# Attention and a linear layer in one kernel: scores and values in four 64x64 array tiles, the causal mask by 64 tokens, fixed score banks, and merged rotations of q and k

## The chip, the core and the metric

The kernel runs on one core of a Trainium2 chip. The metric is the device time of one execution in microseconds; times of several runs are given as their median. The engines of the core are TensorE (PE, with its weight loads shown apart as PEld), VectorE (DVE), ScalarE (ACT), GpSimd (POOL) and SyncE (SP). SP issues most of the DMA transfers, and a transfer that has to wait holds up those behind it on the same queue. PSUM is the memory that matrix products are written into.

## The reference, cut to what matters

The hidden states have 4 sequences of 512 tokens with 1024 features; there are 16 heads of 64. All is float32.

```
q, k, v = x @ Wq.T, x @ Wk.T, x @ Wv.T          # split into 16 heads of 64
q, k = rope(q), rope(k)                          # t * cos + rotate_every_two(t) * sin
scores = where(causal, q @ k.T, -1e9) / sqrt(64) # 512 x 512 per head
attn = softmax(scores) @ v
x = layernorm(x + attn @ Wout.T)
x = layernorm(x + x @ (int8 weight * scale).T)
```

## The kernel before

**Units.** The attention part works in 32 units: a unit u is one sequence b and one pair of heads hp. Units 0 to 15 alternate between sequences 0 and 1 over the eight pairs of heads; units 16 to 31 alternate between sequences 2 and 3, with the pairs of heads in falling order. Weights are therefore loaded and split every second unit.

**Products.** q, k and v of a unit are three products (number 0, 1, 2), transposed: 128 rows (two heads of 64) by 512 tokens. To keep float32 accuracy, operands are split into a high part, a low part and a third part d, and each product is 24 matmuls of 512 columns, called tickets: 16 go into one PSUM bank A (high and low parts), 8 into a bank D. ACT scales A into `tA` (line 295) and DVE adds D to it (line 318): for q and k the result is `raw`, for v it is `v`. The pool `pj` has two banks, so A and D of successive products alternate on them, and D of one product has to wait until the DVE step of line 318 of the product before has read its D.

**Rotation.** For q and k, `swap` (line 249) makes a copy `rot` of `raw` with neighbouring rows exchanged, by two DMAs that SP issues. `rope` then runs three steps on DVE (lines 235, 236, 242): `rot * sin`, `raw * cos`, and their sum into `qk`. Before, these are 512 columns each, once for q and once for k. In units of even number the rotation of the next unit's q is done late in the unit, in odd ones it stands between the softmax parts of the unit (`slot` in `product`); that of k is in the slot "turn".

**One unit of the loop.** The loop over u records, in this order: the scores of u (line 409), their masks and maxima on DVE (lines 427 and 430), the exponentials on ACT (444), the reciprocal of the sums on DVE (452), the normalisation on POOL (458), and 72 tickets, which are product 1 and 2 of unit u + 1 and product 0 of unit u + 2. After 18 tickets come the values of unit u - 1 (`attend`, line 490), copied by ACT out of PSUM (498) and sent by a DMA on ACT's own queue to the DRAM buffer `ao` (499). Row blocks i = 0 to 3 of 128 tokens form three groups: blocks 0 and 1, block 2, block 3. For each group DVE transposes the probabilities in blocks of 32x32 (`turn`, line 463), SP writes them to the DRAM buffer `turned` (464) and reads them back into `prT` in the order that the values need (472). v is turned the same way (`turned_v`, `va`). A read back of `turned` waits until its write has landed.

**Array tiles before.** Scores use tiles of 64 rows by 128 columns: the two heads of a unit lie in the upper and the lower 64 rows, and two such matmuls run side by side. Block i multiplies 128 queries with (i + 1) * 128 keys, so causality is by 128 tokens. Values use tiles of 128 rows by 64 columns, the two heads side by side in the columns. The score tiles and the value tile come from one pool of three buffers of two banks, `pdp`. A mask of 128x128 is added to the diagonal block, by DVE, or on TensorE in the units 0, 30 and 31 (`BUSY`).

**Order.** Within the loop the order of PE, DVE and ACT is that of the program text, written out by hand. Work on SP and POOL is put in order by a scheduler. `later(u, slot, f)` puts work into a named slot of unit u; `run(u, slot)` issues it. The slots of a unit stand in this order: early, between, then, after, first, turn, mid, second, late, end. Splits of weights are DVE steps in the slots between, first and late.

After the loop come the output product (line 199), layer norms, and the last linear layer (676) over 16 tiles of 128 rows.

Of the kernel before, what the change touches and what calls it, by code (L numbers as in the profile page):

```python
# [9 lines left out]
FP = mybir.dt.float32  # L10
# [15 lines left out]
SCALE = 0.125  # L26
MASKED = -3.0e38

# [10 lines left out]
def attention_ffn_kernel(  # L39
# [28 lines left out]
    pds = ExitStack()  # L68
    pdp = pds.enter_context(tc.tile_pool(name="pd", bufs=3, space=PSUM))

    ident = const.tile([P, P], FP, name="ident")
    mask, unit = (const.tile([P, P], BF, name=name) for name in ("mask", "unit"))
    cos_sb = const.tile([P, 2, S], FP, name="cos_sb")
# [6 lines left out]
    for n in (512, 384):  # L80
        nc.tensor.matmul(warm[:, :n], lhsT=sin_sb[:, 0, :P], rhs=sin_sb[:, 0, :n], start=True, stop=True)

    make_identity(nc, ident)
    make_identity(nc, unit)
    nc.gpsimd.memset(mask, 0.0)
    nc.gpsimd.affine_select(
        out=mask,
        in_=mask,
        pattern=[[-1, P]],
        compare_op=ALU.is_ge,  # L90
        fill=MASKED,
        base=0,
        channel_multiplier=1,
    )
    nc.gpsimd.memset(eps_sb, EPS)
# [133 lines left out]
    with tc.tile_pool(name="raw", bufs=2) as rawp, tc.tile_pool(name="qk", bufs=2) as qkp, ExitStack() as heads:  # L229
        def rope(u, k):  # L230

            raw, rot = prod.pop((u, k)), prod.pop(("rot", u, k))
            if u not in qk:
                qk[u] = qkp.tile([P, 2, S], FP, tag="qk", name=f"qk_{u}")
            nc.vector.tensor_mul(rot, rot, sin_sb[:, k, :])
            nc.vector.tensor_mul(raw, raw, cos_sb[:, k, :])
            out = qk[u][:, k, :]
            if k == 0:

                out = out.rearrange("p (i r s) -> p r i s", i=NI, r=R)  # L240
                raw, rot = (t.rearrange("p (r i s) -> p r i s", i=NI, r=R) for t in (raw, rot))
            nc.vector.tensor_add(out, raw, rot)  # L242

        def swap(u, k):

            raw = prod[u, k]
            rot = prod["rot", u, k] = rawp.tile([P, S], FP, tag="rot", name=f"rot_{u}_{k}", bufs=2)
            for p in range(2):
                nc.sync.dma_start(out=rot[p::2, :], in_=raw[1 - p :: 2, :])

        def raw_tile(u, k):
            tag = "v" if k == 2 else "raw"
            t = prod[u, k] = rawp.tile([P, S], FP, tag=tag, name=f"{tag}_{u}_{k}", bufs=1 if k == 2 else 2)
            return t

# [12 lines left out]
        def product(u, k, n):  # L268
# [48 lines left out]
            if n == NT - 1:  # L317
                nc.vector.scalar_tensor_tensor(raw_tile(u, k), ps, -X12, prod["tA"], op0=MUL, op1=ADD)  # L318
                if k < 2:
                    swap(u, k)  # L320
                    slot = ("first" if last else "between" if u % 2 else "late") if k == 0 else "turn"
                    later(u - 1, slot, lambda: rope(u, k))

# [68 lines left out]

        probs, prT, stats, s_ps = {}, {}, {}, {}

        def scores(u):
            nmx = st1.tile([P, 2 * NI], FP, tag="nmx", name=f"nmx_{u}")
            den = st1.tile([P, 2 * NI], FP, tag="den", name=f"den_{u}")
            rden = st1.tile([P, 2 * NI], FP, tag="rden", name=f"rden_{u}")
            stats[u] = nmx, den, rden
            t = qk.pop(u)  # L400
            keys = t[:, 1, :].rearrange("p (r s) -> p r s", r=R)
            for g, blocks in enumerate(GROUPS):
                ps = pdp.tile([P, 2, 512], FP, tag="d", name=f"s_{u}_{g}")
                s_ps[u, g] = ps
                for i, at in blocks:
                    n = (i + 1) * P
                    for j in range(2):
                        rows = slice(j * D, (j + 1) * D)
                        nc.tensor.matmul(  # L409
                            ps[:, j, at : at + n],  # L410
                            lhsT=t[rows, 0, ts(i, P)],
                            rhs=keys[rows, :, : (i + 1) * Q],
                            start=True,
                            stop=u not in BUSY,
                        )
                    if u in BUSY:
                        diag = ps[:, :, at : at + n].rearrange("p a (r s) -> p a r s", r=R)[:, :, :, ts(i, Q)]
                        for j in range(2):
                            nc.tensor.matmul(diag[:, j], lhsT=unit, rhs=mask, start=False, stop=True)

        def maxima(u, g):
            nmx, den, rden = stats[u]
            ps = s_ps[u, g]
            for i, at in () if u in BUSY else GROUPS[g]:
                diag = ps[:, :, at : at + (i + 1) * P].rearrange("p a (r s) -> p a r s", r=R)[:, :, :, ts(i, Q)]
                tri = mask.rearrange("p (r s) -> p r s", r=R).unsqueeze(1).to_broadcast([P, 2, R, Q])
                nc.vector.tensor_tensor(diag, diag, tri, ADD)
            for i, at in GROUPS[g]:
                n = (i + 1) * P
                nc.vector.tensor_reduce(  # L430
                    nmx[:, 2 * i : 2 * i + 2], ps[:, :, at : at + n], AX.X, ALU.max, negate=True
                )

        def softmax(u, g):
            nmx, den, rden = stats[u]
            ps = s_ps.pop((u, g))
            blocks = GROUPS[g]
            pr = prp.tile([P, R, WIDE[g], 2, Q], FP, tag=f"pr{g}", name=f"pr_{u}_{g}")
            probs[u, g] = pr
            for i, at in blocks:  # L440
                n = (i + 1) * P
                for j in range(2):
                    m = 2 * i + j
                    nc.scalar.activation(  # L444
                        pr[:, :, at // P : at // P + i + 1, j, :],
                        ps[:, j, at : at + n].rearrange("p (r k s) -> p r k s", r=R, s=Q),
                        AF.Exp,
                        bias=nmx[:, m : m + 1],
                        accum_out=den[:, m : m + 1],
                    )  # L450
            i0, i1 = blocks[0][0], blocks[-1][0] + 1
            nc.vector.reciprocal(rden[:, 2 * i0 : 2 * i1], den[:, 2 * i0 : 2 * i1])  # L452
            for i, at in blocks:
                n = (i + 1) * P
                for j in range(2):
                    m = 2 * i + j
                    p = pr[:, :, at // P : at // P + i + 1, j, :]
                    nc.gpsimd.tensor_scalar(p, p, rden[:, m : m + 1], 1.0, ALU.mult, ALU.mult)  # L458

        def turn(t, d):  # L460

            t = t.rearrange("p r k j s -> p (r k j s)") if len(t.shape) > 2 else t
            nc.vector.transpose(t, t)  # L463
            nc.sync.dma_start(out=d.rearrange("a (n r) w -> (a n) (r w)", r=R), in_=t)
# [12 lines left out]
        def turn_values(u):  # L477

            rows = turn(prod.pop((u, 2)), turned["v"])
            va[u] = vap.tile([P, NI, R, Q], FP, tag="va", name=f"va_{u}")  # L480
# [3 lines left out]
        def attend(u):  # L484
            b, hp = units[u]
            ps = pdp.tile([P, 2, 512], FP, tag="d", name=f"o_{u}")[:, 0, :]
            t, v = prT.pop(u), va.pop(u)
            for kb in range(NI):
                for j in range(2):
                    nc.tensor.matmul(  # L490
                        ps[j * D : (j + 1) * D, kb * P :],
                        lhsT=v[:, kb, 2 * j : 2 * j + 2, :].rearrange("p a s -> p (a s)"),
                        rhs=t[:, :, 4 * kb : 3 * (NI - 1) + kb + 1 : 3, j, :].rearrange("p a i s -> p i a s"),
                        start=(kb == 0),
                        stop=(kb == NI - 1),
                    )
            o = otp.tile([P, S], FP, tag="ot", name=f"ot_{u}")
            nc.scalar.copy(o, ps)
            nc.scalar.dma_start(out=ao[b][:, hp, :], in_=o)

        with tc.manual_schedule(
# [60 lines left out]
            later(0, "first", lambda: split_w(0))  # L564
            later(0, "late", lambda: (diff_x(0, 3), rope(1, 0)))

# [5 lines left out]
            for u in range(NU):  # L572
# [13 lines left out]
                second = 8 if u < NU - 1 else 6  # L586
                transposes(u, 0)
                take(second)
                transposes(u, 1)
# [17 lines left out]
                run(u, "end")  # L607
            attend(NU - 1)
    pds.close()


    w8p = ctx.enter_context(tc.tile_pool(name="w8", bufs=1))
    wfv = w8p.tile([P, NC, E], FR, name="wf")
    sc32 = w8p.tile([P, E], FP, name="sc32")
# [157 lines left out]
```

## Time and profile before

| | |
|---|---|
| median of 3 runs | 1020.42 us (1020.23 to 1020.58) |
| span of the profiled execution | 1020.7 us |
| PE busy | 999.7 us |
| DVE busy | 852.8 us |
| ACT busy | 389.0 us |
| POOL busy | 201.1 us |
| mean granted TensorE clock | 0.996 |
| data moved | 204.09 MB |

The profiled execution is one run. Its span is taken from its own trace, 0.3 us above the median, so sums of its rows may be set against 1020.7. A line of the timeline gives the start in us, the length, the engine, the source line, the operation and the tiles as output<-inputs; behind it stands in brackets how long the engine had been idle and what released it. The letter q behind an engine's name marks its DMA queue.

The steady units of the loop run from scores to scores in 21.45 us. The first scores begin at 33.4 us. Units 14 and 15, in which the second pair of sequences is split for the first time, take 24.10 and 22.84 us.

### The profile page before, as it was taken

Reading aid. Unit: us, or ns where it says so; the run is one execution under the profiler, and the core shown is the slowest. Engines: PE = TensorE matmul, PEld = TensorE weight load, DVE = VectorE, ACT = ScalarE, POOL = GpSimd, SP = SyncE. Lnnn points to the kernel's source line nnn. Section 1 sums busy time; section 2 is a strip of 40 time slices with the busy share of each in tenths; the row PEclk is TensorE's granted clock in tenths of the full one; section 3 lists DMA queues with packets and bytes.
Section 4 is the critical chain, followed back from the end, with each engine's and each line's share of the span. In section 5 each row is a group of like instructions: output and inputs, shape, how many; then the busy total and the mean of one; then the engine's idle time right before and its main releaser. Section 6 shows DMA issues by size and latency. Waiting matters only on the chain.

```text
span 1020.7 us, 13748 instructions
## 1 busy us (share of the span) xinstructions
PE 999.7 (98%) x4628; PEld 742.0 (73%) x4628; DVE 852.8 (84%) x1246; ACT 389.0 (38%) x841; POOL 201.1 (20%) x283
## 2 busy tenths in 40 slices
PE   9999999999999999999999999999899999999997
PEld 4667777777777667777777777776578888888885
DVE  5998888888888999788898888889877877878776
ACT  4534444354444435445344453445332122121110
POOL 0122332222322322332223322232100000000000
PEclk9999999999999999999999999999999999999999
DMA  7576676767768787576866758688635465564551
GB/s 288 170 233 220 203 234 190 263 195 223 232 193 261 250 254 227 183 253 192 253 210 206 247 173 273 217 250 278 223 108 160 124 160 143 128 168 104 145 103 62
DMA packets 264022, 204.09 MB, mean 200 GB/s; under 512 B 147600, under 2 KB 220304, under 8 KB 263824
## 3 DMA queue, kind: packets, MB, share of 16 engines
q1 hardware_dynamic: 256176, 184.60, 60.0%
q10 hardware_dynamic: 5616, 10.75, 2.9%
q0 software_dynamic: 2160, 7.87, 1.9%
q8 instruction: 37, 0.61, 0.3%
q14 instruction: 33, 0.27, 0.1%
HBM read 112.46 MB, written 73.92 MB: 183 GB/s over the span
## 4 chain that ended last, share of the span: by engine, by line
PE 85%; DMA 5%; issue 4%; DVE 4%; POOL 1%; SPq 0%; ACT 0%; DVEq 0%; POOLq 0%
PE p L276 43%; PE y L199 15%; PE f L676 11%; PE o L490 7%; PE s L409 6%; PE pw L261 2%; DMA turned<-pr 2%; DVE pr L463 1%; POOL pr L458 1%; DMA sx<-in_wo 1%; DMA prT<-turned 1%; DMA raw_x<-in_xT 1%; DVE w_l L219 1%; DMA va<-turned_v 0%; DMA turned_v<-v 0%
## 5 line engine op out<-in xcount | busy, mean ns | idle before, releaser
L458 POOL TENSOR_SCALAR pr<-pr,rden 128x128 f32<-128x128 f32 (+3 forms) x256 | 189.9, 760 | 525.9 <-DVE rden L452 414.5
L276 PE MATMUL p<-x_h,w_h 128*128 128x512 f32 x736 | 290.2, 394 | 0.0
L276 PE MATMUL p<-x_l,w_l 128*128 128x512 f32 x736 | 286.8, 390 | 0.0
L276 PE MATMUL p<-x_d,w_d 128*128 128x512 f32 x736 | 190.9, 395 | 3.1 <-DVE v L318 2.5
L276 PEld LDWEIGHTS p<-x_h,w_h 128*128 128x128 f32 x736 | 138.1, 188 | 50.3 <-issue 22.0
L444 ACT ACTIVATE pr<-s,nmx 128x128 f32<-128x128 f32 (+3 forms) x256 | 131.5, 531 | 112.6 <-DVE nmx L430 107.1
L276 PEld LDWEIGHTS p<-x_d,w_d 128*128 128x128 f32 x736 | 135.5, 188 | 36.4 <-issue 5.1
L276 PEld LDWEIGHTS p<-x_l,w_l 128*128 128x128 f32 x736 | 138.2, 188 | 28.1
L295 ACT ACTIVATE tA<-p 128x512 f32<-128x512 f32 x92 | 55.2, 600 | 218.4 <-PE p L276 218.4
L463 DVE STREAM_TRANSPOSE pr<-pr 128x768 f32<-128x768 f32 (+1 forms) x96 | 99.7, 1057 | 24.4 <-POOL pr L458 23.7
L430 DVE TENSOR_REDUCE nmx<-s 128x2 f32<-128x256 f32 (+3 forms) x128 | 101.9, 820 | 3.0
L199 PE MATMUL y<-x_l,w_l 128*128 128x512 f32 x256 | 100.1, 391 | 2.1 <-DVE w_l L219 2.1
L199 PE MATMUL y<-x_h,w_h 128*128 128x512 f32 x256 | 100.4, 392 | 0.5 <-DVE row L208 0.5
L676 PE MATMUL f<-wf,x1lo 128*128 128x512 f32 x240 | 93.6, 390 | 1.1 <-DVE x1lo L650 1.1
L676 PE MATMUL f<-wf,x1hi 128*128 128x512 f32 x240 | 93.5, 389 | 0.0
L409 PE MATMUL s<-qk 64*128 64x384 f32 (+3 forms) x512 | 80.2, 446 | 1.0 <-DVE qk L242 1.0
L490 PE MATMUL o<-prT,va 128*64 128x256 f32 (+3 forms) x512 | 77.7, 446 | 2.2 <-DMA prT<-turned 1.7
L223 DVE TENSOR_TENSOR w_d<-w_h,w_l 128x1024 fp32r<-128x1024 f32 x60 | 74.0, 1233 | 1.5
L318 DVE SCALAR_TENSOR_TENSOR raw<-p,tA 128x512 f32<-128x512 f32 x61 | 41.8, 686 | 37.1 <-PE p L276 37.0
L490 PEld LDWEIGHTS o<-prT,va 128*64 128x64 f32 x512 | 34.8, 138 | 48.6 <-issue 42.6
L199 PE MATMUL y<-x_d,w_d 128*128 128x512 f32 x256 | 64.9, 393 | 1.6 <-DVE x_d L177 1.2
L409 PEld LDWEIGHTS s<-qk 64*128 64x128 f32 x512 | 41.4, 186 | 22.4 <-issue 11.3
(112 smaller groups left out, 1162.1 us busy)
## 6 DMA issues: line engine op xcount, KB each, us to landing
turned<-pr SPq DMA_DIRECT2D x64, 384.0 KB, 3.4
rot<-raw SPq DMA_DIRECT2D x128, 128.0 KB, 2.8
turned<-pr SPq DMA_DIRECT2D x32, 512.0 KB, 4.5
prT<-turned SPq DMA_DIRECT2D x32, 512.0 KB, 5.2
prT<-turned SPq DMA_DIRECT2D x32, 384.0 KB, 3.9
turned_v<-v SPq DMA_DIRECT2D x32, 256.0 KB, 5.0
va<-turned_v SPq DMA_DIRECT2D x128, 64.0 KB, 2.6
prT<-turned SPq DMA_DIRECT2D x32, 256.0 KB, 3.3
```

The costliest lines, as they stand in the source:

```text
L199: nc.tensor.matmul(ps, lhsT=r[part][:, c, :], rhs=w[part][:, c, :], start=n in (0, 2 * NC), stop=n in (2 * NC - 1, NT - 1),)
L223: nc.vector.tensor_tensor(d, h, l, SUB)
L276: nc.tensor.matmul(ps, lhsT=w[part][:, c, :], rhs=r[part][:, c, :], start=n in (0, 2 * NC), stop=n in (2 * NC - 1, NT - 1),)
L295: nc.scalar.activation(prod["tA"], ps, AF.Copy, scale=1.0 + X12)
L318: nc.vector.scalar_tensor_tensor(raw_tile(u, k), ps, -X12, prod["tA"], op0=MUL, op1=ADD)
L409: nc.tensor.matmul(ps[:, j, at : at + n], lhsT=t[rows, 0, ts(i, P)], rhs=keys[rows, :, : (i + 1) * Q], start=True, stop=u not in BUSY,)
L430: nc.vector.tensor_reduce(nmx[:, 2 * i : 2 * i + 2], ps[:, :, at : at + n], AX.X, ALU.max, negate=True)
L444: nc.scalar.activation(pr[:, :, at // P : at // P + i + 1, j, :], ps[:, j, at : at + n].rearrange("p (r k s) -> p r k s", r=R, s=Q), AF.Ex ...
L458: nc.gpsimd.tensor_scalar(p, p, rden[:, m : m + 1], 1.0, ALU.mult, ALU.mult)
L463: nc.vector.transpose(t, t)
L490: nc.tensor.matmul(ps[j * D : (j + 1) * D, kb * P :], lhsT=v[:, kb, 2 * j : 2 * j + 2, :].rearrange("p a s -> p (a s)"), rhs=t[:, :, 4 * k ...
L676: nc.tensor.matmul(ps, lhsT=part[:, c, :], rhs=wfv[:, c, o], start=(c == 0 and part is hi), stop=(c == NC - 1 and part is lo),)
```

## The change

The order of tokens in each sequence is changed by the host: within a block of 128 tokens they are put into rows of 16 by their number modulo 4, and odd blocks have their two halves exchanged. The host puts the rows of the result back. Then:

- Scores: four tiles of 64x64 (two heads in the rows, two halves of the queries in the columns). Each half of the queries takes only the keys that it needs by steps of 64 tokens.
- Values: four tiles of 64x64 (two halves of the keys in the rows, two heads in the columns). The two halves of the keys give two sums in two banks; ACT copies the first, DVE adds the second (`attended`), and the DMA to `ao` goes to SP's queue.
- The three score buffers are allocated once; the values always use the first.
- Masks: `added` and `bounds`, one for even and one for odd blocks, are built by POOL in token order and moved into place by 32 small DMAs that POOL issues. DVE takes the minimum with `bounds`; in the units of `BUSY` TensorE adds `added`.
- q and k of a unit share one `raw` and one `rot` tile, single-buffered. One rotation over 1024 columns replaces two over 512, in the slot "turn".
- v is transposed by blocks into a new tile under the name of `tA`.
- The identity for the transposes of the last part is made after the loop.

```diff
+    ps_d = [pdp.tile([P, 2, 512], FP, name=f"s_{g}") for g in range(3)]
...
+        for masks, open_value in ((added, 0.0), (bounds, -MASKED)):
+            by_token = maskp.tile([P, 2, P], BF, tag="by_token", name="by_token")
...
+                for c in range(2):
+                    for r in range(4):
+                        at, of = 64 * c + 16 * r, 64 * (c ^ odd) + r
+                        nc.gpsimd.dma_start(out=masks[at : at + 16, odd, :], in_=by_token[of : of + 61 : 4, odd, :])
...
-        def rope(u, k):
+        def rope(u, *ks):
...
-            nc.vector.tensor_mul(rot, rot, sin_sb[:, k, :])
-            nc.vector.tensor_mul(raw, raw, cos_sb[:, k, :])
+            nc.vector.tensor_mul(rot, rot, sin_sb[:, ks, :])
+            nc.vector.tensor_mul(raw, raw, cos_sb[:, ks, :])
+            nc.vector.tensor_add(qk[u][:, ks, :], raw, rot)
...
-                    slot = ("first" if last else "between" if u % 2 else "late") if k == 0 else "turn"
-                    later(u - 1, slot, lambda: rope(u, k))
+                    if k == 1:
+                        later(u - 1, "turn", lambda: rope(u, 0, 1))
...
+                    for c in range(2):
+                        early = i * P + c * D
+                        if i % 2 != c:
+                            pieces = ((0, (i + 1) * P),)
+                        elif c == 0:
+                            pieces = ((0, early + D),)
+                        else:
+                            pieces = ((0, i * P), (early, early + D))
+                        for j in range(2):
+                            rows = slice(j * D, (j + 1) * D)
+                            for s0, s1 in pieces:
+                                nc.tensor.matmul(
+                                    ps[c * D : (c + 1) * D, j, at + s0 : at + s1],
+                                    lhsT=t[rows, 0, early : early + D],
+                                    rhs=t[rows, 1, s0:s1],
...
-                nc.vector.tensor_tensor(diag, diag, tri, ADD)
+                nc.vector.tensor_tensor(diag, diag, tri, ALU.min)
...
+                for h in range(2):
+                    for j in range(2):
+                        rows = slice(h * D, (h + 1) * D)
...
+                        if h == kb % 2:
+                            piece(kb * P, later_blocks(kb))
+                        else:
+                            c = 1 - kb % 2
+                            piece(kb * P + c * D, t[rows, 2 * c : 2 * c + 2, 4 * kb, j, :])
+                            if kb < NI - 1:
+                                piece((kb + 1) * P, later_blocks(kb + 1))
+            o = outs[u] = otp.tile([P, S], FP, tag="ot", name=f"ot_{u}")
+            nc.scalar.copy(o, ps[:, 0, :])
+
+        def attended(u):
+
+            b, hp = units[u]
+            o = outs.pop(u)
+            nc.vector.tensor_tensor(o[:, D:], values.pop(u)[:, 1, D:], o[:, D:], ADD)
+            nc.sync.dma_start(out=ao[b][:, hp, :], in_=o)
...
                 transposes(u, 0)
+                if u:
+                    attended(u - 1)
```

## The prediction

> **What bounds the kernel now.** I read the page first (busy shares, chain by engine), then the chain of waits in order of time, then one steady unit on TensorE, DVE and SyncE, then the two units that are longer than the others.
>
> ```profile
> PE 999.7 (98%) x4628; PEld 742.0 (73%) x4628; DVE 852.8 (84%) x1246; ACT 389.0 (38%) x841; POOL 201.1 (20%) x283
> PE 85%; DMA 5%; issue 4%; DVE 4%; POOL 1%; SPq 0%; ACT 0%; DVEq 0%; POOLq 0%
> ```
>
> ```profile
> 98.28 2.36 PE s L409 x16
> 100.64 4.32 PE p L276 x18
> 104.96 2.31 PE o L490 x16
> 107.27 12.46 PE p L276 x54
> ```
>
> TensorE is busy 98% of the span. The last four lines (start, length, engine) are one unit of the attention loop: 2.36 + 4.32 + 2.31 + 12.46 = 21.45 us, with no gap; scores and values are 4.67 of it, the 72 product tickets the rest. DVE at 84% is the next bound. The view by stretches of two neighbouring units and of the one unit that is far longer (length, busy PE, PEld, DVE, ACT, POOL, granted clock, DMA share, GB/s):
>
> ```profile
> 98.21:119.66 21.45, 21.45 (x105) 15.72 (x105) 17.03 (x26) 7.64 (x22) 6.12 (x8) 1.00 0.76 239
> 119.66:141.11 21.45, 21.45 (x106) 15.72 (x105) 19.39 (x28) 11.63 (x25) 5.45 (x8) 1.00 0.64 206
> 334.13:358.23 24.10, 22.06 (x106) 15.56 (x105) 23.35 (x32) 10.14 (x24) 8.58 (x8) 1.00 0.77 249
> ```
>
> The clock is 1.00 in all three, so the long unit is no matter of the clock. What makes it long shows in its timelines (start, length, engine, line):
>
> ```profile
> 355.45 0.68 DVE L318 SCALAR_TENSOR_TENSOR v<-p,tA 128x512 f32<-128x512 f32 x1
> ```
>
> ```profile
> 354.36 0.39 PE L276 MATMUL p<-x_l,w_l 128*128 128x512 f32 x1
> 356.19 2.11 PE L276 MATMUL p<-x_d,w_d 128*128 128x512 f32 x8 [1.44 <-DVE v L318]
> 358.23 2.43 PE L409 MATMUL s<-qk 64*128 64x128 f32 x16
> ```
>
> Ticket 65, the first of the last eight, reuses the bank that DVE's v evacuation (L318) reads. DVE gets there late, TensorE waits 1.44, and the next unit starts 358.23 - 355.45 = 2.78 us after that evacuation began. This is the law I use: **period = start of the v evacuation within the unit + 2.78**, when it comes late. Without a wait ticket 65 starts 358.23 - 356.19 = 2.04 before the unit's end and 0.74 after the evacuation's start, so the evacuation has until 21.45 - 2.78 = 18.67. In the unit at 119.66 it starts at 137.25, 17.6 into the unit: only 1.1 us of slack. Before it stand these rows of DVE:
>
> ```profile
> 128.72 0.98 DVE L463 STREAM_TRANSPOSE pr<-pr 128x768 f32<-128x768 f32 x1 [0.59 <-POOL pr L458]
> ...
> 132.96 1.18 DVE L219 SCALAR_TENSOR_TENSOR w_l<-w_h,sw 128x1024 fp32r<-128x1024 f32 x1
> 134.18 1.23 DVE L223 TENSOR_TENSOR w_d<-w_h,w_l 128x1024 fp32r<-128x1024 f32 x1
> ...
> 137.25 0.68 DVE L318 SCALAR_TENSOR_TENSOR v<-p,tA 128x512 f32<-128x512 f32 x1
> ```
>
> **TensorE's part.** In scores and in values each array tile streams 1280 columns per pass now, two tiles at once; the change has four tiles of 1152. If four run together, 4.67 becomes 4.67 x 1152/1280 = 4.20: 0.47 us per unit, 15 in 32 units. Two at a time, as these rows have it, would give twice 4.20: +3.7 per unit. I take the gain: two tiles now share the array at no cost, and four need no other resource that a row shows as full. The Trainium skill, "TensorEngine Tiling (Array Packing)", Instruction Overhead, speaks against: it charges some 60 cycles to each matmul and advises not to tile a dimension that is small already. With 40 and 44 instructions in place of 16 and 16, my estimate from that page is that half the gain would be lost; no row here has a 64-column matmul to judge it by.
>
> **DVE's part.** The mask stays the same size. New is one addition (attended, 448 columns out of PSUM) behind the first transposition: by the nearest row, a 512-column product out of PSUM at 675 ns, 0.6 us. In this place DVE waited 0.64 for TensorE anyway, so 0 to 0.6. The rotations merge: two chains of three 512-column steps, 1.93 each (135.32 to 137.25), become one of three 1024-column steps, by the w_d row (1.23, steps of 1.14 to 1.25) 3.53. By busy time DVE is where it was. What counts is the place: **the whole rotation, for q and k, now stands ahead of the v evacuation in every unit**, and it needs the swapped copy of k, which comes by DMA.
>
> **SyncE's part.** This is where I expect the loss. Its queue in the unit at 119.66, and a row of the view of its waits (us in all, times, longest):
>
> ```profile
> 129.73 0.33 SPq L464 DMA_DIRECT2D turned<-pr  x1
> 131.05 1.13 SPq L249 DMA_DIRECT2D rot<-raw  x2
> 132.96 0.93 SPq L472 DMA_DIRECT2D prT<-turned  x2
> 133.98 0.93 SPq L464 DMA_DIRECT2D turned<-pr  x2
> ```
>
> ```profile
> SPq L472 <- DMA turned<-pr: 120.7, 91, 3.4
> ```
>
> The swap of k goes out between the first turned write and its read-back. In the built order of the changed program (26 units: 2 to 13 and 16 to 29) the queue has the turned write, the two read-backs, the attention output (moved here from ACT's queue), and only then the swap. The read-backs wait for the write to land: 120.7 us over 91 waits. So the swap is behind that landing, rotation behind the swap, v behind the rotation, ticket 65 behind v. In the even unit, from its start: the first transposition starts at 9.06 now, held by POOL, which shared its time with a rotation that the change takes away; I take 8.2, the reciprocal's end. Write issued 9.2; landing 2.65 later (usual in these units; 2.33 in odd ones; page median 3.4); read-backs 0.93; output 0.4; swap 1.13; its landing 2.05 (page median 2.8). Sum 16.35. The weight split on DVE is over by 15.3 and hides nothing of it. Rotation 3.53, v at 19.9, period 22.7. In the odd unit the masks start 0.55 later, because behind the late v evacuation DVE still has a weight split, v's transposition and the next raw evacuation; and POOL shares with a split. Its first transposition starts at 9.74 now, then at 10.15, ends 11.1; 2.4 + 0.93 + 0.4 + 1.13 + 2.05 later it is 18.0; v at 21.5, period 24.3. A pair takes 47.0 where it took 42.9: +4.1, and 13 pairs make **+53**. Landings at the page's medians add 1.5 to each unit, landings a little quicker and fully hidden issues take 1 off: +2.5 to +6.5 a pair, 32 to 85 in all. TensorE's 0.47 is already swallowed in this: it lengthens only the wait at ticket 65.
>
> **Start, middle, end.** The masks are now put together by 32 DMAs that POOL issues one after the other; its nearest row, an output write, takes 0.53 to issue and 3.5 to land, so 17 us and the landing, done near 23 (13 if issues are half that, 40 at one us each). The first staged x tile of the second batch shares memory with the masks' source and waits for that; it landed at 13.1 and would at 23 + 6.1 = 29. ACT's split of it (1.06) is ahead of the copy of k (0.59), then swap (1.13 + 2.05) and rotation (3.53): scores of unit 0 at 38 instead of 33.4, +5. DVE's splits of that x are some 13 us late as well, and unit 0 and 1 need them: I take +12 by unit 2, from 5 to 25. Units 14 and 15 have the swap ahead of the read-backs: +0.5 each. The last two units and the identity that is made after the loop: +1, up to 8. Exponentials write runs of 16 instead of 32: taken at nothing, since ACT is at 38%; each us that they cost would add a us to every pair's chain.
>
> **Sum.** 1020.7 is the profiled span, 0.3 over the median of 1020.42. 53 + 12 + 1 + 1 = 67, less 0.3: **1087 us**.
>
> **Rivals.**
> - *Faster: the swap lands in time.* The span would be 1020 - 15 = 1006, or some 1012 with a dearer start. It needs v by 18.2, hence the second swap landed by 14.7; my sums have 16.35 and 18.0, and 15.1 is the point of no change. For it: POOL and DMA latencies would have to fall by 1.7 and 3.3 together. Against it: units 14 and 15, where 1.4 us of lateness came through whole. Chance 0.10, and 0.02 for a draw within 0.2%, about what a measurement of this kernel can tell from no change.
> - *Stall in odd units alone* (the write lands in 1.5, the start hidden): even 21.2, odd 23, +1.3 a pair, 17 + 5: about 1042. For it: some landings of 2 us; against: DMA engines at 0.64 to 0.76 in these units. Chance 0.08.
> - *Four tiles do not run together* (two at a time, or weight loads in a row): PE needs 21.45 + 3.7 = 25.2 in every unit, which is longer than either stalled period: +120 and the start: about 1150. For it: no row with four; against: two already do. Chance 0.05.
>
> The forecast itself has 0.75. The range 1052 to 1120 is the pair's 2.5 to 6.5 with the start's 5 to 25, cut where both would have to be extreme; it leaves out the first rival, most of the second and the third. Faster 0.10, same 0.02, slower 0.88.
>
> **What would show it.** TensorE's row of p with x_d, w_d should wait for v L327 in nearly every unit, 1.5 to 4 us, alternating; the swap's rows should follow the read-backs on SyncE and DVE's rotation should wait for "DMA rot<-raw". Scores and values should take about 4.2 together. POOL's DMAs should end near 23. Wrong: units of 21 us without that wait (the swap is not late), or scores above 3 us (the tiles do not overlap).

## The result, and the profile after

The changed kernel takes 1141.66 us (median of 5 runs, 1136.87 to 1143.76) against 1020.58 (1020.23 to 1021.02): 1.118 times as long, interval 1.1156 to 1.1206. It is slower, as forecast, but by 121 us and not by 67; 1141.66 lies above the stated range of 1052 to 1120. The profiled execution has a span of 1135.1 us and is the fastest of the five.

The page after, first its busy shares and its chain by engine:

```profile
span 1135.1 us, 17114 instructions
PE 1032.7 (91%) x6292; PEld 790.4 (70%) x6292; DVE 855.5 (75%) x1185; ACT 385.8 (34%) x841; POOL 200.9 (18%) x319
PE 37%; issue 26%; DMA 15%; DVE 13%; POOL 5%; SPq 3%; ACT 2%; DVEq 0%; POOLq 0%; ACTq 0%
```

TensorE had 85% of the chain and has 37%. DVE's busy time is what it was (855.5 against 852.8): not more work but later work. The groups of instructions (busy us, mean ns, then idle time of the engine just before them and what ended it) name the two waits:

```profile
L285 PE MATMUL p<-x_d,w_d 128*128 128x512 f32 x736 | 212.0, 427 | 78.4 <-DVE v L327 78.1
L245 DVE TENSOR_TENSOR rot<-rot,sin_sb 128x1024 f32<-128x1024 f32 (+1 forms) x33 | 39.3, 1192 | 87.6 <-DMA rot<-raw 87.6
```

TensorE waits 78 us for the v evacuation, DVE 88 us for the swapped copy. One odd unit of the chain, the unit that starts at 265.69 (start, length, what):

```profile
275.87 0.99 DVE pr L484
...
276.88 2.31 DMA turned<-pr
...
279.24 0.37 SPq L493
...
279.65 0.51 SPq L493
...
280.25 0.45 SPq L546
...
280.80 0.50 SPq L255
...
281.35 2.96 DMA rot<-raw
...
284.44 1.23 DVE rot L245
...
287.97 0.69 DVE v L327
...
288.71 3.24 PE p L285 x8
```

These are the steps of the prediction in their order: transposition, landing of the write, two read-backs, output, swap, its landing, rotation, v, ticket 65, and 288.71 - 287.97 = 0.74 from v to ticket 65. But the last line was not foreseen. Eight tickets took 1.98 us in the same unit where nothing was late; here they take 3.24. The view by stretches (us, busy PE, PEld, DVE, ACT, POOL, clock, DMA share, GB/s) says why:

```profile
242.09:265.69 23.60, 21.56 (x158) 16.64 (x157) 18.67 (x25) 10.60 (x24) 4.08 (x8) 1.00 0.57 179
265.69:287.97 22.28, 19.52 (x149) 15.22 (x148) 16.46 (x24) 5.85 (x19) 6.15 (x8) 1.00 0.65 201
287.97:291.88 3.91, 3.17 (x8) 2.05 (x8) 1.40 (x3) 2.60 (x3) 0.00 (x0) 0.68 0.63 202
291.88:294.00 2.12, 2.12 (x37) 1.83 (x38) 1.47 (x3) 0.00 (x0) 0.00 (x0) 0.78 0.08 24
```

The granted clock is 1.00 through the wait of 3.50 us, and 0.68 and 0.78 in the two stretches behind it. Cut where the clock changes, the same time reads:

```profile
288.71:289.38 0.67, 0.67 (x3) 0.58 (x4) 0.67 (x1) 0.63 (x2) 0.00 (x0) 1.00 0.75 249
289.38:292.79 3.41, 3.41 (x23) 2.38 (x25) 0.71 (x2) 1.97 (x2) 0.00 (x0) 0.50 0.47 164
292.79:294.00 1.21, 1.21 (x26) 0.92 (x22) 0.78 (x2) 0.00 (x0) 0.00 (x0) 1.00 0.09 34
```

The clock is half, 0.50, for 3.41 us, beginning 0.67 us after ticket 65 starts. In single instructions, tickets start 427 ns apart there and not some 230. In the row for the even unit before (the first of the four), where the idle time was 2.04 us, the clock stays at 1.00.

Where the 114.4 us between the two spans lie, by the starts of the scores: 14.5 before unit 2 (91.25 against 76.77), 92.6 in the 26 units with the swap behind the read-backs, 3.2 in units 14 and 15, 4.1 from unit 30 to the end. Among the 26 units, twelve take over 0.3 us longer than the start of their v evacuation plus 2.78; these twelve are exactly the units in which the trace records a stretch at half clock.

### The profile page after: what moved, and what is told of

It reads as the page before. It is cut to its first block, busy times and chain, and to the rows that moved or that the text cites. A ratio compares the mean times of both kernels' runs of the same rounds, so it can differ in the third digit from the quotient of the medians.

```text
span 1135.1 us, 17114 instructions
## 1 busy us (share of the span) xinstructions
PE 1032.7 (91%) x6292; PEld 790.4 (70%) x6292; DVE 855.5 (75%) x1185; ACT 385.8 (34%) x841; POOL 200.9 (18%) x319
## 3 DMA queue, kind: packets, MB, share of 16 engines
q10 hardware_dynamic: 1008, 2.36, 0.6%
## 4 chain that ended last, share of the span: by engine, by line
PE 37%; issue 26%; DMA 15%; DVE 13%; POOL 5%; SPq 3%; ACT 2%; DVEq 0%; POOLq 0%; ACTq 0%
PE y L208 13%; PE f L728 10%; PE p L285 9%; DMA turned<-pr 6%; DMA rot<-raw 5%; POOL pr L479 4%; DVE pr L484 3%; PE s L424 3%; DVE rot L245 2%; DVE raw L246 2%; PE s L518 2%; ACT pr L465 1%; DMA turned_v<-vt 1%; DVE v L327 1%; SPq L493 1%
## 5 line engine op out<-in xcount | busy, mean ns | idle before, releaser
L479 POOL TENSOR_SCALAR pr<-pr,rden 128x128 f32<-128x128 f32 (+3 forms) x256 | 171.8, 691 | 638.7 <-DVE rden L473 462.0
L285 PE MATMUL p<-x_d,w_d 128*128 128x512 f32 x736 | 212.0, 427 | 78.4 <-DVE v L327 78.1
L285 PEld LDWEIGHTS p<-x_d,w_d 128*128 128x128 f32 x736 | 143.9, 202 | 125.4 <-DVE v L327 90.7
L245 DVE TENSOR_TENSOR rot<-rot,sin_sb 128x1024 f32<-128x1024 f32 (+1 forms) x33 | 39.3, 1192 | 87.6 <-DMA rot<-raw 87.6
L424 PE MATMUL s<-qk 64*64 64x64 f32 (+5 forms) x1280 | 82.3, 395 | 0.0
L424 PEld LDWEIGHTS s<-qk 64*64 64x64 f32 x1280 | 59.9, 151 | 30.4 <-issue 19.0
L518 PE MATMUL s<-prT,va 64*64 64x64 f32 (+4 forms) x1408 | 77.8, 351 | 2.3 <-DMA prT<-turned 2.3
L518 PEld LDWEIGHTS s<-prT,va 64*64 64x64 f32 x1408 | 53.9, 134 | 29.7 <-issue 22.2
```

The lines of the kernel that those rows point to most:

```text
L245: nc.vector.tensor_mul(rot, rot, sin_sb[:, ks, :])
L285: nc.tensor.matmul(ps, lhsT=w[part][:, c, :], rhs=r[part][:, c, :], start=n in (0, 2 * NC), stop=n in (2 * NC - 1, NT - 1),)
L424: nc.tensor.matmul(ps[c * D : (c + 1) * D, j, at + s0 : at + s1], lhsT=t[rows, 0, early : early + D], rhs=t[rows, 1, s0:s1], start=s0 == 0 ...
L518: nc.tensor.matmul(ps[j * D : (j + 1) * D, h, at : at + n], lhsT=lhsT, rhs=rhs, start=kb == 0 and at == h * D, stop=kb == NI - 1,)
```

## The experiments

The theory: the swap is late because of its queue; v is late because it stands behind the rotation; and long waits halve TensorE's clock. The rivals: more work on DVE, small tiles that cost more, a rotation that is long by being merged. Medians and sums of units below are those of the 26 units 2 to 13 and 16 to 29.

**e1_swap_act.** The swap on another queue.

```diff
-                nc.sync.dma_start(out=prod["rot", u][p::2, k, :], in_=raw[1 - p :: 2, :])
+                nc.scalar.dma_start(out=prod["rot", u][p::2, k, :], in_=raw[1 - p :: 2, :])
```

> The changed kernel with one edit: the DMAs that swap rows of q and k go out on ACT's queue, so they no longer stand behind the read-backs of turned on SP. Queue theory (the swap is late because it is queued behind a landing): second swap lands 15.7 us into odd units, in even ones before the weight split ends at 15.3; v evacuation at 19.3 and 18.9; units 22.0 and 21.7; waits at ticket 65 below 1.2 us and no 427 ns tickets; with start and end as in the changed kernel 1050 us, 1042 to 1060. Rival (DVE's merged rotation ahead of v or the small tiles are themselves too long, whatever the queue): still above 1100.

Measured 1050.22 us (1048.48 to 1052.06), ratio 1.0296 (1.0279 to 1.0314). The median unit is 21.8 (even) and 21.4 (odd). TensorE's waits:

```profile
PE p L285 <- DVE v L327: 11.3, 18, 2.2
```

From 78.1 to 11.3 us with four tiles and merged rotation as they were: the rival that those are too slow by themselves falls. Moving the swaps to another queue takes 91 of the 121 us away. One wait is longer than expected (2.2 us in unit 14, where 1.2 was the limit), and the trace has half clock behind it.

**e2_v_first.** The rotation behind v.

```diff
-                        later(u - 1, "turn", lambda: rope(u, 0, 1))
+                        plan.setdefault((u - 1, "late"), []).insert(0, lambda: rope(u, 0, 1))
```

> The changed kernel with one edit: the merged rotation stands behind the v evacuation (first in the slot late) and not ahead of it; the swap stays behind the read-backs. Theory (ticket 65 waits for v only because the rotation is ahead of it): the wait for v goes; the rotation ends 20.3 us into even units, before the next scores, and about 22 to 23 into odd ones, so a wait of 1 to 2 us for qk at the scores of every second unit takes its place; 1060 us, 1045 to 1075. Rival (the late swap holds up everything, order on DVE is immaterial): the same wait moves to the scores in full, 1110 or more.

Measured 1069.14 us (1067.82 to 1070.21), ratio 1.0475 (1.046 to 1.0491). (Here and in the next run the last unit is rotated after its tables have been overwritten with rows of x; its values differ, its instructions do not.) The wait has moved to the scores, as forecast:

```profile
PE s L424 <- DVE qk L247: 25.7, 18, 2.4
```

The median even unit takes 21.31, the odd one 23.35. The late swap still shows, but mainly in every second unit, and the rival, by which the wait moves in full, falls.

**e3_both.** Both edits.

> Both edits together: swap on ACT's queue, rotation behind the v evacuation. Theory: no wait is left in a steady unit, which takes 21.45 less the 0.17 that scores and values save, 21.3; start +14.5, middle and end as in the changed kernel: 1037 us, 1030 to 1044. Rival (four tiles or the addition of the two sums cost elsewhere): steady units above 21.6, over 1045.

Measured 1042.12 us (1041.98 to 1047.81), ratio 1.0225 (1.0198 to 1.0251). Two neighbouring units by stretches:

```profile
192.62:213.89 21.27, 21.27 (x157) 16.73 (x156) 18.79 (x27) 7.41 (x22) 6.14 (x8) 1.00 0.71 223
213.89:235.16 21.27, 21.27 (x157) 16.73 (x156) 17.63 (x24) 11.50 (x25) 4.09 (x8) 1.00 0.72 225
```

TensorE has no gap in these two, and a unit takes 21.27 where it took 21.45. Seven of the 26 units take 21.4 to 22.6, so that the sum of the 26, 558.1, is no less than the 557.7 of before. The effects do not add (91 and 73 alone, 100 together), since both edits shorten the same wait. What is left above 1020 is outside these units: the start (8.6 us up to unit 2, not the 14.5 that was expected), units 14 and 15 (1.8), and the stretch from unit 30 to the end (8.7), where unit 30 took 35.5 us against 24.8.

**e6_fill and e8_fill2.** To test the clock alone, idle matmuls ahead of ticket 65, which shorten TensorE's idle time and change nothing in what it waits for.

```diff
+            if n == 2 * NC and k == 0 and 2 < u:
+                for i in range(12 if u % 2 else 6):      # e6: range(6), WD[0][0] and r[0]
+                    nc.tensor.matmul(ps_d[0][:, 1, :], lhsT=w[2][:, i % NC, :], rhs=r[2][:, i % NC, :], start=True, stop=True)
```

> The changed kernel with six idle matmuls of 512 columns (into a score bank that nobody reads then) ahead of ticket 65 of units 1 to 29, 1.4 us, shorter than the shortest wait there: TensorE idles less and waits for v just as long. Clock theory (after a wait of some 2.6 us or more TensorE's granted clock is halved for a while, which costs the 14.1 us that units take beyond v + 2.78, and makes the next scores late): 1112 us, 1105 to 1122, with the clock of the page near 0.99 and units of v + 2.78 throughout. Rival (the slow tickets come from contention, not from idling): no gain or a loss, 1135 to 1145.

Measured 1183.74 us (1180.22 to 1186.39), ratio 1.1597 (1.1572 to 1.1621). The experiment missed its aim: the operands of the idle matmuls were a weight part that ACT writes late in odd units, so they waited themselves, and made the idle time longer:

```profile
PE s L283 <- ACT w_h L223: 70.9, 13, 6.5
```

With operands that ticket 65 needs anyway:

> As e6_fill, with operands that ticket 65 needs too (x_d, w_d), so that the idle matmuls do not wait for a weight split themselves; six in even units (1.4 us), twelve in odd ones (2.8 us). Clock theory: idle time falls below 2 us everywhere, the clock stays whole, units are v + 2.78, the scores after odd units take 2.2 and not 3.2; 1112 us, 1104 to 1125. Rival (the slow tickets are not due to idling): 1135 to 1150.

Measured 1121.08 us (1119.99 to 1124.67), ratio 1.0987 (1.0962 to 1.1011): 20.6 us less than the changed kernel, with more work on TensorE. The mean clock of the changed kernel, and of this one:

```profile
core 0: 1135.1 us, clock 0.963
```

```profile
core 0: 1119.2 us, clock 0.989
```

In the 26 units the trace has no stretch at half clock any more. The time beyond v + 2.78 falls from 14.1 us to 0.1, and the sum of the units from 650.3 to 630.1. So the clock costs 20.2 us there, by one execution of each kernel: 14.1 directly, and the rest mostly because scores at half clock (3.2 us and not 2.2) make the next unit's masks late (the first write of even units goes out at 9.19 in the mean, in the changed kernel at 9.56). This is shown, not only argued, since the wait for v stayed. Outside the 26 units the experiment is less clean: in unit 14 the swap lands late, ticket 65 waits 4.95 us, the clock is halved, and the unit takes 30.0 us against 23.9 in the changed kernel.

**e7_split.** The merge undone: separate `raw` and `rot` tiles for q and k, q rotated in the slots of before.

```diff
-                    if k == 1:
-                        later(u - 1, "turn", lambda: rope(u, 0, 1))
+                    slot = ("first" if last else "between" if u % 2 else "late") if k == 0 else "turn"
+                    later(u - 1, slot, lambda: rope(u, k))
```

> The changed kernel with the merge undone: q and k have raw and rot tiles of their own, q is rotated between or late as in the kernel before, k alone in the slot turn; the swaps stay on SP behind the read-backs. Theory (queue and merge add up): the swap of k still lands 16.8 and 18.5 us into even and odd units, but only 1.93 of rotation stands between it and v, not 3.53, so v starts at 18.8 and 20.5 and units take 21.5 and 23.3; waits stay below some 2.3 us, so the clock stays; 1066 us, 1055 to 1080. Rival (the loss is the merge's alone): steady units of 21.3 and some 1040. Rival (the loss is the queue's alone): no more than 1.6 a unit saved, 1095 or more.

Measured 1090.78 us (1086.04 to 1091.52), ratio 1.0674 (1.0648 to 1.07); the expectation was 25 us too low. Odd units that keep the clock take mostly 23.3 to 23.6, as expected (23.3). Two things were overlooked. With q's rotation back between the softmax parts (in even units; the section on the kernel before has even and odd the wrong way round: at 119.66, an even unit, it starts 6.06 us into the unit, in odd ones some 14), POOL's normalisation in even units takes 5.5 us again and not 4.1, so the first write goes out at 10.0 and not 9.2, and these units take 22.3, not 21.5. And idle times of 2.0 to 2.9 us, most of which I had thought safe, halved the clock in seven odd units (24.7 to 26.0). Where the swap is late, undoing the merge gains 51 us. The first rival falls, with units far above 21.3. The second is nearer than the theory: the 26 units gain 1.5 us each, within its 1.6, and the total is only 4 us below its 1095. The run alone does not settle it. What the runs show together is the sum of the 26 units above the 557.7 of before: 92.6 with both the late swap and the merged rotation ahead of v, 53.6 with the late swap alone (e7_split), 7.9 with the merged rotation alone (e1_swap_act), 0.4 with neither (e3_both). The queue is the larger part, and the two make each other worse.

**e9_four and e10_two.** All edits together, with the masks' source in memory that nothing early needs, and the last unit's q and k rotated one after the other ahead of the tables' reloading; e10_two also has the values in two tiles, as before.

```diff
-    with tc.tile_pool(name="mask", bufs=2) as maskp:
+        mask_src = rawp.tile([P, S], FP, tag="tA", name="mask_src")
...
+                    if last:
+                        later(u - 1, "rope" if k else "first", lambda: rope(u, k))
+                    elif k == 1:
+                        later(u - 1, "rope", lambda: rope(u, 0, 1))
...
+                run(u, "rope")
                 if u == NU - 2:
                     rows_of_tables()
```

> The changed kernel with all that the runs so far point to: swaps on ACT's queue; rotation behind v, in a slot ahead of the reloading of the tables; q and k of the last unit rotated one after the other as before; the masks' source in memory that is not shared with the staged x. Theory: the first scores at about 33.5 again, steady units of 21.27, units 14 and 15 together 1 to 2 us above before, unit 30 near 25; 1017 us, 1013 to 1022. Rival (the masks' DMAs hold up the start by their traffic, not by the shared memory): +8, 1025.

Measured 1025.49 us (1023.9 to 1027.76), ratio 1.0047 (1.0032 to 1.0061).

> As e9_four, but the values in two tiles of 128 by 64 as in the kernel before, with no second sum, no addition on DVE, and the output's DMA on ACT's queue. If the four-tile values are worth nothing (the traces have 2.325 against 2.304 us), this is the same or a little faster: steady units 21.25, units 14 and 15 shorter by up to 1.2 together, 1016 us, 1012 to 1021. If four tiles do save time in the values that only the trace's edge hides, it is slower by up to 6.

Measured 1019.46 us (1018.83 to 1020.01), ratio 0.9987 (0.9976 to 0.9997): the only version here with a median below that of the kernel before. The 0.1% is too little to be called faster.

The first load of the second batch's x on SP, in the changed kernel and in e9_four:

```profile
23.81 1.28 SPq L174 DMA_DIRECT2D sx<-in_xT  x3
```

```profile
6.91 0.35 SPq L155 DMA_DIRECT2D sx<-in_xT  x1
```

The first scores begin at 40.74 and at 33.56 (before: 33.38; e3_both, which has the other edits but still shares the memory: 40.52), while the masks' DMAs are still issued until 24 us in e9_four. So the first scores were late through the shared memory, not through the DMAs' traffic: the rival of e9_four falls at this place. Still e9_four missed its own number by 8.5 us: some units take 21.4 to 22.2 and not 21.27, units 14 and 15 take 1.8 more than before, unit 30 1.0 more, and the stretch from unit 31's start to the end is 2 us longer. In e10_two every steady unit takes 21.25:

```profile
204.01:225.26 21.25, 21.25 (x129) 16.13 (x129) 17.02 (x23) 11.40 (x25) 4.08 (x8) 1.00 0.71 224
```

The 26 steady units gain 5.2 us there (552.5 against 557.7); units 14 and 15 give back 0.9, unit 30 1.5.

**e11_order and e12_ao_act.** Why four tiles bring the values nothing.

```diff
-                for h in range(2):
+                for h in (kb % 2, 1 - kb % 2):
```

> As e9_four, with the two halves of the keys issued in turn: in every second block of keys the half with the longer piece goes first. In the trace of e9_four no matmul of the values starts between 0.52 and 0.91 us, while the lower tiles have finished 448 columns and the upper ones still stream 512. If tiles wait there for the program's order, the values take 2.325 less some 0.2 us, 2.1 to 2.2, steady units 21.05 to 21.15 and the total 1020 to 1023, against 1025.5. Rival (the small pieces and their weight loads are the cost, in whatever order): 2.3, steady units 21.27, 1024 to 1027.

Measured 1024.63 us (1023.53 to 1026.4), ratio 1.0034 (1.0024 to 1.0043). The values of one unit and the ticket after them, in e9_four and in e11_order:

```profile
430.57 2.40 PE L520 MATMUL s<-prT,va 64*64 64x512 f32 x44
432.89 1.66 PE L285 MATMUL p<-x_d,w_d 128*128 128x512 f32 x6
```

```profile
430.59 2.24 PE L520 MATMUL s<-prT,va 64*64 64x512 f32 x44
432.76 1.66 PE L285 MATMUL p<-x_d,w_d 128*128 128x512 f32 x6
```

From 2.32 to 2.17: tiles did wait for the program's order. Most steady odd units take 21.12. But the total falls by less than 1 us, which the ranges of the runs do not tell from nothing, since more even units take 21.5 to 23. I put these down to the read-backs, which lie behind the output's DMA on SP:

> As e11_order, with the DMA of the attention output on ACT's queue, as in the kernel before and in e10_two. In e11_order a dozen units take 21.2 to 23.0 and not 21.12, because the values wait for the last read-back of the unit before, which lands 6.6 us into the unit in one of them; on SP it stands behind the output's DMA, which waits for the addition. If that is the cause, nearly all steady units take 21.12 and the total is 1018, 1015 to 1021, against 1024.6. Rival (the addition on DVE alone delays the transpositions): no gain, 1023 to 1026.

Measured 1025.06 us (1019.17 to 1029.27), ratio 1.0033 (1.0012 to 1.0054). This is inconclusive: the median even unit fell from 21.5 to 21.15, but some units still take 21.8 to 22.9, the total is the rival's, and the runs scatter by 10 us. What disturbs the units of the versions with two sums stays open.

## Why the prediction was right and wrong

The direction and the mechanism of the wait were right, and each link stands in the chain above; what the mechanism lacked is the clock. With a whole clock (e8_fill2) the first write of the even units goes out at 9.2 (forecast 9.2), of the odd ones at 11.2 (11.1); it lands 2.4 later in the mean (2.65 and 2.4); v + 2.78 holds wherever the clock is whole. Of the rivals, "the swap lands in time" is what e1 builds, but its price was too good: with the second swap landed 14.4 us into a usual even unit, the merged rotation still starts behind the weight split, at 15.5, and the units take 21.8 and 21.4, not 21. "Four tiles do not run together" is false: scores fell from 2.36 to 2.17.

The forecast failed at three steps.

- **The law beyond its row.** "period = start of the v evacuation within the unit + 2.78" was read from a unit that waited 1.44 us and used for waits of 1.5 to 4. It said "The clock is 1.00 in all three, so the long unit is no matter of the clock", which is true of that unit and says nothing of longer waits. The clock was thus put at nothing. Missing term: 20.2 us in the 26 units, of which e8_fill2 is the measurement. With it, waiting costs more than the wait. With a whole clock a pair costs 5.6 us more than before, within the stated 2.5 to 6.5, and the kernel 1121 us, at the upper end of the range; with the clock as granted a pair costs 7.1.
- **The size of the chain.** With a whole clock (e8_fill2) v starts at 20.35 and 22.55, where the sums had 19.9 and 21.5. That is 0.45 + 1.05 a pair, 19.5 us over 13 pairs. Two terms of the sum were too small. From the landing of the write to the first issue of the swap the sum had 0.93 + 0.4 = 1.33; the means of even and odd units are 1.79 and 1.65. From there to the landing of the second swap it had 1.13 + 2.05 = 3.18; the means are 3.33 and 3.61. The landing alone took 2.80 and 3.05, near the page's median of 2.8, where I took the typical 2.05 of the kernel before; that this cost no more was luck, for a landing is timed from the start of its issue, and the sum set it behind both issues. The 53 forecast, 20.2 and 19.5 make 92.7, and 92.6 was measured; but since both differences are taken from e8_fill2, this is bookkeeping and no second proof.
- **The small terms.** The start cost 14.5 (forecast 12). The wait for memory shared with the masks was its larger cause, as said: unit 2 starts at 85.39 in e3_both and at 76.52 in e9_four, 8.9 us. The rest is mostly unit 1, which took 27.16 us and in e3_both 21.49; the forecast had put all that comes after the first scores, 7 of its 12, down to DVE's late splits of x. Since e3_both leaves these as they are, in unit 1 it was the swap and the rotation, and the near hit of the total is in part luck. Part of the start is clock again: 12 matmuls after a wait of 3.6 us took 8.44 us at a clock of 0.50, where they took 5.31 before. Units 14 and 15 took +3.2 (forecast +1), the end +4.1 (+1).

The sum was also set against the span alone: in each run that lists both, the time is 1.8 us above the span. So the profiled execution of before was near 1022.5, 2 above the median and not 0.3. The forecast stays where it is, since it is the median and a sum of differences.

On TensorE the gain was 0.19 in the scores and -0.02 in the values, 0.17 in place of 0.47. The Trainium skill, "TensorEngine Tiling (Array Packing)", Instruction Overhead, from which the prediction estimated, without showing how, that half of the gain would be lost, was nearer than my sum. But the cost is not only one per instruction: e11_order has the same instructions and gains 0.15 by their order, which fits what "TensorE: Matmul & The Clock Gate", Part 2, says of matmuls that stay in program order.

## What to carry to other kernels

When a step is moved ahead of an evacuation that a bank waits for, follow its inputs back through the DMA queue: a transfer that is ready may stand behind one that waits for a landing, and another queue costs one word. Where such a wait cannot be avoided, let it fall behind the evacuation and not ahead of it. And a forecast of a stall on TensorE needs a term for the clock: a wait read off at 1.4 us does not tell what one of 3 us costs. Here a wait was free of it as long as TensorE idled less than some 1.8 us.

## What the runs showed of the hardware that was not expected

How long a wait must be to halve the clock does not follow from its length alone. Of TensorE's idle times over 0.3 us between the first and the last scores of all twelve kernels, so many had half clock begin during them or in the 6 us after them: none of 139 below 1.5 us, 5 of 33 from 1.5 to 2 us, 9 of 16 from 2 to 2.5 us, 36 of 41 above. A wait of 1.8 us can halve the clock, and one of 3.35 need not.

The record of the clock in the traces shows what decides. Between the first and the last scores the clock changes only at points of a grid of 3.41 us, and a stretch at half clock lasts 3.41 us or a multiple. Cut into windows at this grid, the windows at whole clock in which TensorE idled less than 1.75 us were never followed by half clock (1379 of them), 6 of 23 with 1.75 to 2 us were, and all 44 with more. (The ends of matmuls are modelled, so the idle times are not exact.) So it is the idle time inside one window that counts. The wait of 3.35 us that ends at 188.84 in the changed kernel is divided by the grid into 1.49 and 1.86 and left the clock whole; the one of 1.96 us that ends at 648.22 in e7_split lies in one window and halved it. The Trainium skill, "TensorE: Matmul & The Clock Gate", Part 1, has the clock halved after an idle window of some 3.4 us; the grid here has that length, but a window that was idle for a little over half of it was enough, and the measurement decides.

The 64x64 tiles do run four at a time: 40 matmuls of scores take 2.17 us, where two at a time would, as an estimate from the 2.36 us of before, take 2.36 x 2 x 1152/1280 = 4.25. How much they gain depends on the order in which the tiles' pieces are issued.
